# Sums of squares on TensorE, and more products around the start of the output stage, in a two-layer state-space kernel

## The chip, the cores and the metric

The kernel runs on one core of a Trainium2 chip. The metric is the device time of one execution in microseconds (us), as the median of several runs. A core has five engines with a queue each: TensorE (PE, with its weight loads as PEld), VectorE (DVE), ScalarE (ACT), GpSimd (POOL) and SyncE (SP, which here issues most DMAs). Each engine takes its instructions in the order of the program. An instruction that waits for another engine holds back all that stands behind it in its own queue.

## The reference, cut to what matters

The input is `x` of shape (8, 64, 64, 96): 8 images. Two layers follow each other, each of the same form, with different details in the scan.

```python
# layer: x + ref(_gn(x), ...)
xz = x @ in_proj_w                       # 96 -> 2 * 192: x_val and z
x_val = silu(conv3x3_depthwise(x_val) + conv_b)
y = sum over four directions of scan(x_val)   # rows, columns, and both reversed
m = jnp.mean(y, -1, keepdims=True)            # over the 192 channels
v = jnp.var(y, -1, keepdims=True)
y = (y - m) * rsqrt(v + eps) * ln_g + ln_b
return (y * silu(z)) @ out_proj_w             # 192 -> 96, then added to x
```

What the change touches is the last part: mean and variance over 192 channels, the gate with `silu(z)`, and the output product.

## The kernel before, in words

Channels lie on partitions: the 192 channels are two halves of 96 partitions, positions (4096 per image) lie along the free axis. For each image `b` the program runs `scan_rows` (the four scans of layer 1, in 384 sets of 128x1024, with the convolutions of the next image worked in beside them), and then `between(b)`, which calls `out_phase`, the output stage. From image 1 on, `scan_rows` ends with the short unit: 6 sets of 128x960 that belong to layer 2 of the image before. Their results are collected on PE in `collect` (line 1025, 32 small products for a set) and taken off by ACT in `release` (line 1068). PSUM holds one bank for these sums (`pacc`), so that a group's products wait until ACT has taken the group before. The last image's stage is called from `finish`, and a final one of 8 chunks ends the program.

`out_phase` works on chunks of 512 positions: 8 of layer 1's image and, from image 1 on, 8 of layer 2's image before, so 16 chunks in a stage. It is a software pipeline written out by hand. In step k each entry `(stage, lag)` of the tuple `order` (line 1654) does its part for chunk k - lag:

- `first_sum` (lag 0, POOL, line 1620): `y_sum`, the sum of the two halves, 96x512.
- `mean` (lag 1, PE, line 1544): a product with `w["avg"]`, 96x96 of 1/192, which sums over the channels and leaves the mean on all partitions of the PSUM tile `ps_mean`.
- `centre` (lag 1, DVE, line 1636): subtracts it in place.
- `square` (lag 2, ACT, line 1599): squares of both halves to `sq` (2 buffers).
- `second_sum` (lag 2, POOL, line 1627): adds the two halves of `sq` to `squares` (4 buffers).
- `variance` (lag 3, PE, line 1577, at every fourth chunk): four products with `w["avg"][:, :32]`, one for each chunk of a group, into 32 partitions each of the bank `ps_var`.
- `roots` (ACT, line 1650 for the table load, 1651 and 1652) and `newton` (DVE, lines 1537 to 1539), for each group of four: the reciprocal root.
- `row` (lag 8, PE, line 1554): spreads it over the partitions; `scale` (lag 8, DVE, line 1640).
- `gates` (lag 7, PE, line 1567): two products for z into `ps_z` (2 banks); `silu` (lag 7, ACT, line 1616).
- `affine` (lag 9, ACT line 1605, DVE line 1608), `product` (lag 9, POOL, line 1632), `project` (lag 10, PE, line 1589), `end` (lag 10, DVE, line 1752 or 1677), `store` (lag 11).

Within a step each engine takes its parts in the order of the tuple. Behind them come the stages of a plan: the next image's first projections (`ps_proj`, line 577), its first step sizes (`ps_dt`, line 628 on PE; lines 640 to 657 on ACT; three adds of 96x1024 on DVE, lines 661 to 663; a product on POOL, line 607), the scaling and patching of layer 2's sums (ACT line 1772, DVE line 1776), and statistics (DVE line 174). Small banks hold `ps_mean`, `ps_proj`, `ps_dt` and `ps_zb`: two banks in turn.

The first `y_sum` of a stage lies where tiles of the scan lay, and so it waits until PE has read the last set's `out`.

Of the kernel before, what the change touches and what calls it, by code (L numbers as in the profile page):

```python
# [9 lines left out]
F32 = mybir.dt.float32  # L10
AF = mybir.ActivationFunctionType
ALU = mybir.AluOpType
# [4 lines left out]
NB, HH, WW, C = 8, 64, 64, 96  # L17
L = HH * WW
NH = 2
# [4 lines left out]
MM = 512  # L24
SUB = T // MM
P = 128
Q = 4
GC = 32
GS = P // GC
NG = C // GC  # L30
NS = N // GS
# [3 lines left out]
PE_ROWS = 40  # L35
AHEAD = 5
SETS = 4
PER = NG * NS
HEAD = 160
HN = K * HEAD  # L40
# [12 lines left out]
def two_ss2d_layers(ctx: ExitStack, tc: tile.TileContext, t: dict, out: bass.AP):  # L53
# [13 lines left out]
    nc = tc.nc  # L67
# [19 lines left out]
    w = {}  # L87
# [20 lines left out]
    for i in range(L // MM):  # L108
        at = slice(i * MM, (i + 1) * MM)
# [315 lines left out]
    def scan_rows(xc, y, parts, plan, rows, beside):  # L425

        with (
            tc.tile_pool(name="loads", bufs=2, side="right") as loads,
            tc.tile_pool(name="piece", bufs=1) as piece,
            tc.tile_pool(name="work", bufs=2) as work,
            tc.tile_pool(name="pslot", bufs=2, space=PSUM) as pslot,  # L440
            tc.tile_pool(name="pdrive", bufs=1, space=PSUM) as pdrive,
            tc.tile_pool(name="pacc", bufs=1, space=PSUM) as pacc,
            tc.tile_pool(name="pmisc", bufs=1, space=PSUM) as pmisc,
        ):
            units, jobs, sets, x_dbl = parts
            total = len(sets)
            whole = sum(not s["unit"]["short"] for s in sets)
            plan = plan(pmisc)
            with tc.manual_schedule():
                state = None  # L450
                arena = piece.tile([P, 4 * T], F32, name="arena")
                ring = work.tile([P, SETS, T], F32, name="set", bufs=1)
                tables = loads.tile([P, 2 * NS, T], F32, name="bc_rep", bufs=1)
                cums = cycle(tables[:, i, :] for i in (1, 3, 2, NS + 1))
                plan.setdefault(-1, []).insert(0, lambda: low_rows(x_dbl, units[1], rows))
                for n in range(-AHEAD, max(total + 4, max(plan, default=0) + 1)):
                    at = lambda i: sets[n + i] if 0 <= n + i < total else None
                    m, j = divmod(n + 1, PER)
                    if j == 0 and 0 <= m < len(jobs):

                        stages = []
                        if m + 2 < len(jobs):
                            prepare = short_ready if jobs[m + 2]["unit"]["short"] else ready_by_time
                            stages += prepare(xc, x_dbl, jobs[m + 2], arena, pmisc)
                        if m % NH == 1 and m // NH + 2 < len(units):
                            unit = units[m // NH + 2]
                            project = short_projection if unit["short"] else projection
                            stages += project(xc, x_dbl, unit, rows, pmisc)
                        for step, stage in stages:
                            plan.setdefault(n + step, []).append(stage)  # L470
                    fetch(at(AHEAD), False, loads, None)
                    if at(0) and at(0)["unit"]["nth"] == 0 and at(0)["first"]:
                        state = piece.tile([P, D // GC * NS], F32, name="state0", bufs=2)
                    advance_set(at(0), state, ring, tables)
                    fill(at(1), pslot)
                    drive(at(2), pdrive)
                    release(at(-4), y, beside)
                    keep_state(at(-1))
                    gate(at(1), pdrive)
                    early(at(1), True, ring)  # L480
                    read_out(at(-1), work)
                    early(at(2), False, ring)
                    replicate(at(4), x_dbl, tables, ("b", 0), ("b", 1))
                    replicate(at(3), x_dbl, tables, ("c", 0), ("b", 3))
                    replicate(at(2), x_dbl, tables, ("c", 1), ("b", 2))
                    replicate(at(1), x_dbl, tables, ("c", 2))
                    replicate(at(0), x_dbl, tables, ("c", 3))
                    replicate_short(at(4), "b", tables[:, 0, :])
                    if n + 4 == whole:
                        fetch(at(4), True, loads, cums)  # L490
                    replicate_short(at(3), "c", tables[:, NS, :])
                    if n + 3 != whole:
                        fetch(at(3), True, loads, cums)
                    late = (n + 1) % NS == 0
                    if not late:
                        collect(at(-3), xc, y, pacc)
                    for stage in plan.pop(n, []):
                        stage()
                    if late:
                        collect(at(-3), xc, y, pacc)  # L500
                assert not plan
# [512 lines left out]
    def collect(s, xc, y, pacc):  # L1014
# [32 lines left out]
        for acc, at in parts:  # L1047
# [6 lines left out]
                skip_group_check=True,  # L1054
            )

    def release(s, y, beside):

        if not s or s["i"] < NS - 1 and not s["unit"]["short"]:
            return  # L1060
        unit, h, g = s["unit"], s["group"]["h"], s["group"]["g"]
        if unit["short"]:
            if h == g == 0:
                ys_far[unit["b"]] = dram.tile([NH, P, NG * HEAD], F32, name="ys_far", bufs=2)
            if g == 0:
                unit["y"] = beside.tile([P, MM], F32, tag="conv_out", name="y_short")
            part = unit["y"][:, g * HEAD : (g + 1) * HEAD]
            nc.scalar.mul(part, s["group"]["acc"][:, :HEAD], 0.5)
            if g == NG - 1:
                nc.sync.dma_start(ys_far[unit["b"]][h], unit["y"][:, : NG * HEAD])  # L1070
            return
        n = T // Q
        for a in range(Q):
            yk = positions(
                y[GC * g : GC * (g + 1), h, :], unit["column"], unit["t0"] + a * n, n
            )
            acc = s["group"]["acc"][GC * a : GC * (a + 1), :n]
            nc.scalar.copy(yk, like(acc, unit["column"]))  # L1078
# [397 lines left out]
    def out_phase(*streams, plan=None, brief=None):  # L1476
# [9 lines left out]
        with (  # L1486
# [8 lines left out]
            n = len(streams) * chunks  # L1495
            brief = brief or pool
# [8 lines left out]
            held = [{} for _ in range(n)]  # L1505
# [35 lines left out]
            def mean(c):  # L1541
                held[c]["mean"] = pmm.tile([P, MM], F32, tag="mm", name="ps_mean")
                ps = held[c]["mean"][:C, :]
                nc.tensor.matmul(ps, w["avg"], held[c].pop("sum"), start=True, stop=True)  # L1544

            def row(c):

# [22 lines left out]
            def variance(c):  # L1570

                if c % Q < Q - 1:
                    return
                group = groups[c // Q]
                group["var"] = pvar.tile([P, MM], F32, name="ps_var")
                for q in range(Q):
                    nc.tensor.matmul(
                        group["var"][GC * q : GC * (q + 1), :],
                        w["avg"][:, :GC],
                        held[c - Q + 1 + q].pop("squares"),  # L1580
                        start=True,
                        stop=True,
                        skip_group_check=True,
                    )

            def project(c):
                held[c]["out"] = po.tile([P, MM], F32, name="ps_out")
# [7 lines left out]
                    )  # L1595

            def square(c):
                held[c]["sq"] = brief.tile([C, NH, MM], F32, name="sq", bufs=2)
                nc.scalar.activation(held[c]["sq"], part(c), AF.Square)  # L1599

            def affine(c):
# [16 lines left out]
            def first_sum(c):  # L1618
                held[c]["sum"] = brief.tile([C, MM], F32, name="y_sum", bufs=2)
                nc.gpsimd.tensor_tensor(  # L1620
                    held[c]["sum"], part(c)[:, 0, :], part(c)[:, 1, :], ALU.add
                )

            def second_sum(c):
                sq = held[c].pop("sq")
                held[c]["squares"] = brief.tile([C, MM], F32, name="squares", bufs=Q)
                nc.gpsimd.tensor_tensor(  # L1627
                    held[c]["squares"], sq[:, 0, :], sq[:, 1, :], ALU.add
                )

            def product(c):
# [16 lines left out]
            def roots(group):  # L1648
# [3 lines left out]
                nc.scalar.activation(group["r"], group["r"], AF.Exp, scale=-0.5)  # L1652

            order = (
                (load, 6), (mean, 1), (row, 8), (gates, 7), (variance, 3), (project, 10),
                (square, 2), (affine, 9), (silu, 7), (store, 11),
                (first_sum, 0), (second_sum, 2), (product, 9),
                (centre, 1), (scale, 8), (end, 10),
            )
            with tc.manual_schedule():  # L1660
# [302 lines left out]
    with rotating():  # L1963
        ps = psum.tile([P, T], F32, tag="ps", name="ps_flag")
# [96 lines left out]
```

## Time and profile before

| what | value |
|---|---|
| runs | 11935.63, 11943.43, 11960.0 us; median 11943.43 us |
| profiled execution | 11940.1 us, span 11938.2 us |
| busy share of the span | DVE 91%, POOL 89%, ACT 76%, PE 73% |
| granted PE clock over the span | 0.757 of full speed |
| `squares` on POOL (line 1627) | 128 instructions, 175.7 us |
| `ps_var` on PE (line 1577) | 256 records, 48.9 us |
| `ps_mean` on PE (line 1544) | 256 records, 190.7 us |

The profiled execution is read as one run, 3.3 us under the median. A product of these shapes stands in the trace as two records of TensorE, each with a weight load ahead of it. The clock column (PEclk) is the share of full TensorE clock that was granted in a stretch; in this kernel it changes between 0.50 and 1.00 only. An idle time in brackets behind a row names the engine's instruction that ended it.

The eight output stages that follow the scans, from the first `y_sum` to the next scan's first set, take about 100 us (image 0), 140.5 us (images 1 to 5), 145 us (image 6) and 170 us with its tail (the last image); the final one of 8 chunks takes 70 us.

### The profile page before, as it was taken

The page shows a single profiled execution, that of the slowest core. Times are in us where ns is not written, and L with a number is a line of the kernel's source. Part 1 is how long each engine was busy: PE and PEld are TensorE (multiplying, and loading weights), DVE is VectorE, ACT ScalarE, POOL GpSimd, SP SyncE. Part 2 cuts the span into 40 slices and gives each one's busy share as a digit, 9 for nine tenths or more (in the row PEclk, how much of TensorE's full clock was granted, in tenths as well). Part 3 has the DMA queues.
Part 4 walks back from the last instruction along what each step waited for, and adds up shares of the span by engine and source line. Part 5 has one row for each costly group of instructions (what it writes and reads, how often), then busy time and mean ns, then how long its engine had stood idle before and what let it go on. Part 6 is the DMA issues. An engine that isn't in the chain of part 4 may idle for free. (4 is left out here: it accounts for less than half of the span.)

```text
span 11938.2 us, 146996 instructions
## 1 busy us (share of the span) xinstructions
PE 8683.2 (73%) x50950; PEld 3939.2 (33%) x50950; DVE 10805.3 (91%) x6095; ACT 9034.2 (76%) x14768; POOL 10622.2 (89%) x4799
## 2 busy tenths in 40 slices
PE   6865578776777777776787777877777776886557
PEld 2332233332333323333233332333233332333222
DVE  8999899997999979999799997999879998899985
ACT  6777678786787777877778777787777877777775
POOL 6999889996999979999799987999879998799984
PEclk7776677777778777778777777777778777777667
DMA  4444344444445545445454445444544545444442
GB/s 132 154 165 156 127 163 167 164 156 155 157 165 166 169 140 171 161 159 168 138 171 164 169 150 158 162 159 167 166 146 166 168 158 168 139 159 164 157 151 64
DMA packets 670703, 1862.39 MB, mean 156 GB/s; under 512 B 186728, under 2 KB 201486, under 8 KB 669949
## 3 DMA queue, kind: packets, MB, share of 16 engines
q1 hardware_dynamic: 662781, 1840.30, 46.6%
q10 hardware_dynamic: 7168, 12.59, 0.3%
q8 instruction: 405, 6.64, 0.2%
q14 instruction: 349, 2.86, 0.1%
HBM read 1539.34 MB, written 313.28 MB: 155 GB/s over the span
## 5 line engine op out<-in xcount | busy, mean ns | idle before, releaser
L1012 POOL TENSOR_TENSOR out<-set,bc_rep 128x1024 f32<-128x1024 f32 x3120 | 7318.1, 2368 | 622.4 <-DVE set L996 529.8
L996 DVE TENSOR_TENSOR_SCAN set<-decay,state,set 128x1024 f32<-128x1024 f32 x2304 | 5323.3, 2340 | 310.0 <-ACT decay L943 164.4
L943 ACT ACTIVATE decay<-dt_rep,w_a 128x1024 f32<-128x1024 f32 x3072 | 3420.1, 1114 | 1295.0 <-DVE set L996 1290.9
L1048 PE MATMUL acc<-out,w_gather 128*32 128x256 f32 x24576 | 2396.1, 517 | 23.9 <-POOL out L1012 23.6
L1115 PE MATMUL ps_conv<-edged,taps 96*96 96x512 f32 (+1 forms) x4032 | 2196.7, 688 | 19.2 <-DVE arena L869 10.8
L969 POOL TENSOR_TENSOR set<-dtu_rep,bc_rep 128x1024 f32<-128x1024 f32 (+1 forms) x816 | 1965.5, 2409 | 49.5 <-DMA dtu_rep<-dtu_short 27.5
L996 DVE TENSOR_TENSOR_SCAN set<-decay,set 128x1024 f32<-128x1024 f32 x768 | 1731.2, 2281 | 132.4 <-ACT decay L943 73.6
L981 DVE TENSOR_TENSOR set<-drive,bc_rep 128x2048 f32<-128x2048 f32 x768 | 1743.5, 2270 | 36.5 <-DMA bc_rep<-x_dblr 25.8
L731 PE MATMUL ps_sp<-w_eye,arena 128*96 128x128 f32 x7680 | 1130.6, 310 | 595.5 <-ACT arena L743 500.3
L1039 PE MATMUL acc<-map,w_eye 96*32 96x256 f32 x4608 | 577.3, 584 | 1317.5 <-ACT map L1078 855.9
L1078 ACT COPY map<-acc 32x256 f32<-32x256 f32 x3072 | 1473.8, 480 | 69.9 <-PE acc L1048 29.4
L1048 PEld LDWEIGHTS acc<-out,w_gather 128*32 128x32 f32 x24576 | 877.7, 140 | 1401.8 <-issue 1038.1
L731 PEld LDWEIGHTS ps_sp<-w_eye,arena 128*96 128x96 f32 x7680 | 980.4, 145 | 905.2 <-ACT arena L743 619.4
L697 PE MATMUL ps_dt<-w_dtw,x_dbl 7*128 7x96 f32 x3840 | 820.4, 378 | 570.9 <-ACT arena L743 457.3
L1115 PEld LDWEIGHTS ps_conv<-edged,taps 96*96 96x96 f32 (+1 forms) x4032 | 699.9, 188 | 1286.8 <-issue 1226.8
L697 PEld LDWEIGHTS ps_dt<-w_dtw,x_dbl 7*128 7x128 f32 x3840 | 715.9, 275 | 816.3 <-ACT arena L743 526.3
L983 DVE TENSOR_TENSOR set<-drive,bc_rep 128x1024 f32<-128x1024 f32 x768 | 921.9, 1200 | 23.4 <-DMA bc_rep<-x_dblr 12.0
L961 ACT COPY drive<-dtu_rep 128x1024 f32<-128x1024 f32 x768 | 777.9, 1013 | 112.4 <-DMA dtu_rep<-dtu_far 84.9
L708 ACT ACTIVATE arena<-ps_dt 128x384 f32<-128x384 f32 x480 | 235.5, 491 | 558.6 <-PE ps_dt L697 543.8
L1039 PEld LDWEIGHTS acc<-map,w_eye 96*32 96x32 f32 x4608 | 104.1, 125 | 1639.8 <-ACT map L1078 1002.9
L607 POOL TENSOR_TENSOR arena<-arena,map 96x1024 f32<-96x1024 f32 x240 | 634.7, 2644 | 7.3 <-ACT arena L743 7.2
L1007 ACT COPY state<-set 128x1 f32<-128x1 f32 x2304 | 422.2, 183 | 6.8
(207 smaller groups left out, 7910.9 us busy)
## 6 DMA issues: line engine op xcount, KB each, us to landing
dt_rep<-dt_far SPq DMA_DIRECT2D x768, 512.0 KB
dtu_rep<-dtu_far SPq DMA_DIRECT2D x768, 512.0 KB
bc_rep<-x_dblr SPq DMA_DIRECT2D x512, 512.0 KB
bc_rep<-x_dblc SPq DMA_DIRECT2D x512, 512.0 KB
dt_far<-arena SPq DMA_DIRECT2D x240, 384.0 KB
dtu_far<-arena SPq DMA_DIRECT2D x240, 384.0 KB
xc_far<-conv_out SPq DMA_DIRECT2D x224, 192.0 KB
dt_rep<-dt_short SPq DMA_DIRECT2D x48, 480.0 KB
```

Of the source, the lines that this page charges most:

```text
L697: nc.tensor.matmul(job["ps"][:, j, :], unit["x_dbl"][: R + 1, at : at + P], w["dtw0"][:, k, h * C : (h + 1) * C], start=True, stop=True,)
L731: nc.tensor.matmul(job["ps"][:C, j * P : (j + 1) * P], job[name][:, s * BLOCKS + j, :], w["whole_eye"], is_transpose=True, start=i == 0, s ...
L943: nc.scalar.activation(s["decay"], s["group"]["dt"], AF.Exp, scale=rate)
L961: nc.scalar.copy(s["group"]["drive"], s["group"]["dtu"])
L969: nc.gpsimd.tensor_tensor(s["buf"], s["group"]["dtu"], b, ALU.mult)
L981: nc.vector.tensor_tensor(ring[:, :2, :], drive, tables[:, :2, :], ALU.mult)
L983: nc.vector.tensor_tensor(s["buf"], s["group"]["drive"], unit["b", i], ALU.mult)
L996: nc.vector.tensor_tensor_scan(ordered(s["buf"], unit), ordered(s["decay"], unit), ordered(s["buf"], unit), 0.0 if unit["nth"] == 0 else s ...
L1012: nc.gpsimd.tensor_tensor(s["out"], s["buf"], s["unit"]["c", s["i"]], ALU.mult)
L1048: nc.tensor.matmul(acc, w["gather"], s["out"][:, at : at + n], start=False, stop=s["i"] == NS - 1, skip_group_check=True,)
L1078: nc.scalar.copy(yk, like(acc, unit["column"]))
L1115: nc.tensor.matmul(job["ps"][:C, :], taps[l][:k, h, tap, :], edged[:k, tap // 3 : tap // 3 + rows, tap % 3 : tap % 3 + WW], start=tap == 0 ...
```

## The change

It has four parts. `second_sum` is dropped: the variance's products take both halves of `sq` and add them in PSUM, 8 products for a group instead of 4, and `sq` gets 4 buffers. `variance` moves to the front of PE's step, ahead of `mean`, `row` and `gates`. For the first six chunks of every output stage the product of `mean` is made a second time, into a bank of `ps_z` that nobody reads. And a new function `warm` makes three products of 128x128 by 128x512 from a set's `out`, after the last whole set has been advanced: in the last three steps in which sets are collected, once for each of the last three sets.

```diff
+WARM = 6
...
                     if not late:
                         collect(at(-3), xc, y, pacc)
+                    if n >= total:
+                        warm(at(-3), pmisc)
                     for stage in plan.pop(n, []):
                         stage()
                     if late:
...
+    def warm(s, pmisc):
+
+        if not s:
+            return
+        ps = pmisc.tile([P, MM], F32, tag="mm", name="ps_warm")
+        for _ in range(NS - 1):
+            nc.tensor.matmul(ps, w["whole_eye"], s["out"][:, :MM], start=True, stop=True)
...
             def mean(c):
                 held[c]["mean"] = pmm.tile([P, MM], F32, tag="mm", name="ps_mean")
                 ps = held[c]["mean"][:C, :]
-                nc.tensor.matmul(ps, w["avg"], held[c].pop("sum"), start=True, stop=True)
+                total = held[c].pop("sum")
+                nc.tensor.matmul(ps, w["avg"], total, start=True, stop=True)
+                if c < WARM:
+                    again = pz.tile([P, MM], F32, name="ps_z")[:C, :]
+                    nc.tensor.matmul(again, w["avg"], total, start=True, stop=True)
...
+                for h in range(NH):
+                    for q in range(Q):
+                        nc.tensor.matmul(
+                            group["var"][GC * q : GC * (q + 1), :],
+                            w["avg"][:, :GC],
+                            held[c - Q + 1 + q]["sq"][:, h, :],
+                            start=h == 0,
+                            stop=h == NH - 1,
+                            skip_group_check=True,
+                        )
                 for q in range(Q):
-                    nc.tensor.matmul(
-                        group["var"][GC * q : GC * (q + 1), :],
-                        w["avg"][:, :GC],
-                        held[c - Q + 1 + q].pop("squares"),
-                        start=True,
-                        stop=True,
-                        skip_group_check=True,
-                    )
+                    del held[c - Q + 1 + q]["sq"]
...
-                held[c]["sq"] = brief.tile([C, NH, MM], F32, name="sq", bufs=2)
+                held[c]["sq"] = brief.tile([C, NH, MM], F32, name="sq", bufs=Q)
...
-            def second_sum(c):
-                sq = held[c].pop("sq")
-                held[c]["squares"] = brief.tile([C, MM], F32, name="squares", bufs=Q)
-                nc.gpsimd.tensor_tensor(
-                    held[c]["squares"], sq[:, 0, :], sq[:, 1, :], ALU.add
-                )
...
             order = (
-                (load, 6), (mean, 1), (row, 8), (gates, 7), (variance, 3), (project, 10),
+                (load, 6), (variance, 3), (mean, 1), (row, 8), (gates, 7), (project, 10),
                 (square, 2), (affine, 9), (silu, 7), (store, 11),
-                (first_sum, 0), (second_sum, 2), (product, 9),
+                (first_sum, 0), (product, 9),
```

## The prediction

> **What bounds the kernel now.** I read the page's shares first: DVE 91%, POOL 89%, PE 73% at a granted clock of 0.757. These are averages; the scans, which the change leaves alone, are DVE's and POOL's. So I took the timeline around the stage that follows image 1's scans, first `y_sum` at 2828.97 us, and ask there what ends each wait. Clock and work by stretch, cut where the clock changes (columns: stretch, its length, then busy us of PE, PEld, DVE, ACT, POOL with instructions, granted clock, DMA share, GB/s):
>
> ```profile
> 2801.00:2835.10 34.10, 11.91 (x206) 7.20 (x199) 19.04 (x18) 22.19 (x47) 26.26 (x14) 0.50 0.66 209
> 2835.10:2841.90 6.80, 6.17 (x15) 1.60 (x13) 3.65 (x3) 3.37 (x4) 5.01 (x5) 1.00 1.10 217
> 2842.00:2859.00 17.00, 12.84 (x24) 3.48 (x24) 7.88 (x8) 12.69 (x17) 8.25 (x7) 0.50 0.82 203
> ...
> 2873.32:2889.70 16.38, 16.38 (x26) 4.16 (x27) 9.15 (x10) 9.11 (x12) 9.72 (x6) 0.50 0.25 75
> 2889.70:2920.50 30.80, 28.68 (x79) 9.75 (x77) 27.95 (x40) 27.84 (x38) 22.87 (x15) 1.00 0.24 74
> 2920.50:2930.70 10.20, 9.70 (x13) 2.88 (x14) 9.44 (x10) 4.76 (x7) 6.00 (x4) 0.50 0.20 59
> ```
>
> The stage lasts 139 us, 55 of them at half clock. PE is the bound where it is busy all the time (2873 to 2931), DVE at 2862 to 2873. A half-clock product takes 2.02 us (two records of 0.85), a full-clock one 1.02 (0.43). Now the timeline at the start and in two later steps (start, length, engine, line, work, idle before):
>
> ```profile
> 2823.60 1.08 PE L1025 MATMUL acc<-out,w_gather 128*32 128x160 f32 x32 [0.51 <-ACT y_short L1068]
> 2826.06 1.08 PE L1025 MATMUL acc<-out,w_gather 128*32 128x160 f32 x32 [1.37 <-ACT y_short L1068]
> 2827.64 1.08 PE L1025 MATMUL acc<-out,w_gather 128*32 128x160 f32 x32 [0.51 <-POOL out L1012]
> 2828.97 2.48 POOL L1620 TENSOR_TENSOR y_sum<-map 96x512 f32<-96x512 f32 x2 [1.46 <-PE acc L1025]
> 2830.28 2.02 PE L1544 MATMUL ps_mean<-y_sum,w_avg 96*96 96x512 f32 x2 [1.55 <-POOL y_sum L1620]
> ...
> 2848.87 1.94 PE L1577 MATMUL ps_var<-squares,w_avg 96*32 96x512 f32 x8
> 2850.93 1.26 POOL L1627 TENSOR_TENSOR squares<-sq 96x512 f32<-96x512 f32 x1 [4.42 <-PE ps_var L1577]
> 2850.95 0.69 ACT L1651 ACTIVATE r<-ps_var,eps_ln 128x512 f32<-128x512 f32 x1 [2.46 <-PE ps_var L1577]
> ...
> 2866.71 2.17 DVE L662 TENSOR_TENSOR ln<-ln,z 96x1024 f32<-96x1024 f32 x1
> 2867.76 2.24 POOL L1627 TENSOR_TENSOR squares<-sq 96x512 f32<-96x512 f32 x1
> ...
> 2884.89 1.26 POOL L1627 TENSOR_TENSOR squares<-sq 96x512 f32<-96x512 f32 x1 [6.17 <-PE ps_var L1577]
> ```
>
> The first `y_sum` follows 0.25 us behind PE's last read of `out`: the stage hangs on PE there. The variance stops both ACT and POOL.
>
> **When the clock changes.** From the trace I cut time into the 3.41 us steps in which the clock record moves, and took for each the share of the 128x128 array in use (active rows times columns, times streaming time). After a half-clock step with share 0.7 or more and PE busy 85% or more, the next was at full clock 267 times of 267; with share 0.45 to 0.6 and busy under 96%, 26 of 275. A full-clock step with share under 0.24 was followed by full clock 4 times of 435, with 0.4 or more 972 of 972. So dense products bring the clock back soon, and thin ones lose it even without a gap.
>
> The Trainium skill, TensorE: Matmul & The Clock Gate, Part 1, says that about 3.4 us of sustained work free the clock and one idle window of that length takes it back. The trace differs: 16.38 busy us of 16.38 stayed at 0.50, and the clock fell at 2842 behind a step with no gap over 0.4 us. By the rule the clock would hold from 2835 to the idle stretch at 2851, so the second means would be cost alone (six, 0.86 us each, 5 us an image), and the stretch from 2873 would lose 3 to 7 us to half clock in either kernel.
>
> **1. The idle products, images 1 to 7.** In the changed program's order six of them stand between the fourth group of `collect` (ends 2824.68) and the fifth, three behind the sixth, and the first `y_sum` now waits for the last of these, since it lies where `out` lay. Six are 12 records: 10.2 us at half clock, 5.2 at full. They fill the array, so the clock should come after 2.7 to 6.1 us, say 4.4: 4.4 + (10.2 - 4.4)/2 = 7.3. The fifth group then starts at 2832.1 instead of 2826.06, +6.0; a hole of 1.37 is already taken off. Groups five and six take 2.66 from start to end now and some 1.75 at full clock; three more products add 2.6 and a wait of 0.1. `y_sum` comes at 2836.6 instead of 2828.97: **+7.6** (bounds: full clock at once +5.5; never +13.9). Behind the products wait ACT's last two `y_short` and the whole stage; DVE is idle then anyhow.
>
> **2. Image 0** has no short unit: three groups of products stand between sets that arrive 2.3 us apart, and push the last `collect` and ACT's copies by about +4.
>
> **3. Inside the stage, from the first `y_sum` on.** *Steps 0 to 6.* PE is at full clock, but up to the last `ps_zb` it streams ten products and four more second means one behind the other, 12 us from 1.3: `ps_zb` ends at 13.3, where it ends at 13.5 now. `variance` follows the second `ps_dt`: 17.0 to 19.1 (16 records at full clock, twice 1.06) instead of 19.9 to 21.8. But with 4 buffers `square` of chunk 4 must wait until the variance has read chunk 0, and the table load stands behind it: 19.1 + 1.05 + 1.28 + 1.3 puts the end of the root at 22.8 instead of 23.3. **-0.5.** The idle gap before chunk 6's mean stays at 4 us, so the clock falls again.
> *Steps 7 to 9.* `squares` is gone from POOL; the three adds of lines 661 to 663 (1.48 + 2.17 + 2.17, beside POOL) should take 1.22 each, as the same add took at 2924.85 without it: **-2.1**.
> *Step 10.* The variance's 16 records cost 3.9 us at half clock instead of 1.94, ahead of mean, row and gates, and `square` of chunk 8 with `affine` behind it on ACT wait for them. POOL no longer waits 6.17 us with `product` behind. The eight dense half-clock products should bring the clock back at 48 us after the first `y_sum`; now it comes at 60.7. PE would be 5.5 us early at the first `project`; ACT becomes the bound, at the next `silu` 2.0 us early, and its waits of the next 28 us sum to 3.3. I take -5 in all by step 13.
> *Steps 14 and 18.* Variance ahead of `gates` puts `silu` and the root back by the added 1.06 each: +2.1. The half-clock stretch at 2920 costs PE about 4.5; its cause, a PE gap of 3.1 us behind DVE, shrinks to 2.3, which saves the clock in about one case of three: -1.4. Sum: -5 + 2.1 - 1.4 = **-4** (bounds: +1 if the clock comes back no sooner, -12 if PE stays at full clock through, since 25 of its 55 half-clock us are bound by it).
>
> SP's queue keeps its order; its late loads hide behind steps 0 to 5. The removed 175.7 us of POOL are worth what stands above, no more: POOL waits in the stage.
>
> **Sum.** Images 1 to 6: 6 x (7.6 - 4) = 22. Image 7: 7.6 - 2 = 5.6; its stage runs at full clock from 22.6 us on, so there is less to win. Image 0: 4 - 4 = 0. Final stage, 8 chunks, no idle products: its second means at half clock delay `y_sum` (which waits for them, 1.7 each), its POOL alternation ends: 0. Together +27 on the profiled 11940.1: 11967; the median lies 3.3 above, so **11970**.
>
> **Rivals.** *The clock holds (faster).* The inner gain is 12, not 4: 7 x (7.6 - 12) = -31, 11913. For it: PE bounds 2873 to 2931. Against it: DVE's 5.8 us of adds and the gap after step 6 empty PE. It decides from an inner gain of 11. *The head start is all that changes (slower).* The added variance and second means eat the gains: 7 x 7.6 + 4 = +57, 12000. For it: PE is 93% busy at full clock from 2889 to 2920. *The idle products do not raise the clock,* so the change doesn't do what it says: 7 x 13.9 and no inner gain, +97, 12040. Against it: 267 of 267.
>
> **How the numbers follow.** About 0.2%, 24 us, is what a measurement can tell from no change. Chances: forecast 0.40, clock holds 0.25, head start alone 0.28, no clock 0.07. The forecast lies just past the edge, so four tenths of it count as no change, as does a quarter of the faster case and an eighth of the third: faster 0.19, same 0.26, slower 0.55. The range runs from the faster rival, 11913, to near the last, 12035; the forecast's own is 11945 to 12000.
>
> **What would show it.** In the changed profile: the first `y_sum` some 7.6 us later behind the fourth group of `collect`, with `ps_warm` as its releaser; `square` waiting for `ps_var`; lines 661 to 663 near 1.22; full clock by 50 us into the stage. I am wrong if the stage from first `y_sum` to the next scan shrinks by 10 us or more, or if the idle products take under 5 us of path.

## The result, and the profile after

The changed kernel takes 12012.31 us (median of 4 runs, 11998.8 to 12027.06), the kernel before 11939.53 us on the same chip (11930.0 to 11960.0). The ratio is 1.0059 with a 95% interval of 1.0041 to 1.0077: slower by 0.6%, 73 us. The profiled execution took 12011.98 us, its span is 12009.9 us, 71.7 more than before.

Where the 71.7 us lie is read from both traces with the same division of each of the nine output stages. The *head* goes from the end of the last scan to the start of the first `mean` on PE, the *body* from there to the next scan's first set (or to the program's end), and the *rest* is the scans. Summed over the stages:

| us | before | after | difference | predicted |
|---|---|---|---|---|
| head | 53.7 | 111.1 | +57.3 | +57 |
| body | 1264.9 | 1276.8 | +11.9 | -30 |
| rest | 10619.6 | 10622.1 | +2.5 | 0 |
| half clock between first `y_sum` and next scan | 529 | 399 | -130 | less |

The whole head start was predicted to within 1 us; the gain inside the stage did not come. The loss of the body is uneven: the stages of images 1 and 3 take 6.6 and 5.7 us more, those of images 2, 4 and 5 stay within 0.7 us of the kernel before. The timeline of the changed kernel at the stage behind image 1's scans, with the columns as before (start, length, engine, line, work, idle before and what ended it):

```profile
2817.97 1.08 PE L1028 MATMUL acc<-out,w_gather 128*32 128x160 f32 x32 [0.51 <-ACT y_short L1079]
2818.98 4.13 PE L1066 MATMUL ps_warm<-out,w_eye 128*128 128x512 f32 x6
2823.26 2.81 PE L1066 MATMUL ps_warm<-out,w_eye 128*128 128x512 f32 x6 [0.15 <-PE ps_warm L1066]
2826.01 0.66 PE L1028 MATMUL acc<-out,w_gather 128*32 128x160 f32 x32
2827.20 0.66 PE L1028 MATMUL acc<-out,w_gather 128*32 128x160 f32 x32 [0.54 <-ACT y_short L1079]
2827.80 2.84 PE L1066 MATMUL ps_warm<-out,w_eye 128*128 128x512 f32 x6
2830.86 2.48 POOL L1638 TENSOR_TENSOR y_sum<-map 96x512 f32<-96x512 f32 x2 [8.99 <-PE ps_warm L1066]
...
2849.11 3.64 PE L1593 MATMUL ps_var<-sq,w_avg 96*32 96x512 f32 x16
2852.81 1.06 ACT L1617 ACTIVATE sq<-map 96x1024 f32<-96x1024 f32 x1 [6.19 <-PE ps_var L1593]
2856.55 1.27 POOL L1638 TENSOR_TENSOR y_sum<-map 96x512 f32<-96x512 f32 x1 [7.92 <-PE ps_z L1559]
...
2877.08 3.64 PE L1593 MATMUL ps_var<-sq,w_avg 96*32 96x512 f32 x16
2880.74 1.06 ACT L1617 ACTIVATE sq<-y 96x1024 f32<-96x1024 f32 x1 [5.44 <-PE ps_var L1593]
```

From the fourth `collect` group's end to the first `y_sum` pass 11.8 us (2819.05 to 2830.86); before it was 4.3 (2824.68 to 2828.97). Six idle products run from 2818.98 to 2826.07, with the clock rising on the way, groups five and six take 0.66 us each, three more products follow, and `y_sum` waits for the last. The first two of the stage's four variance groups take 3.64 us, the half-clock price of 16 records, and ACT's `square` stands behind each. In the whole kernel before, POOL's `squares` waited 75.7 us for the variance; now ACT's `square` waits 70.0 us for it, so the wait has changed its engine rather than gone. The waits of POOL's `y_sum` in the page's groups (busy us, mean ns, then idle before and what ended it):

```profile
L1638 POOL TENSOR_TENSOR y_sum<-map 96x512 f32<-96x512 f32 x72 | 90.7, 1264 | 198.1 <-PE ps_z L1559 122.3 <-PE ps_warm L1066 55.3 <-DMA y<-xc_far 7.9
L1593 PE MATMUL ps_var<-sq,w_avg 96*32 96x512 f32 x512 | 83.1, 779 | 0.0
L1066 PE MATMUL ps_warm<-out,w_eye 128*128 128x512 f32 x144 | 81.5, 710 | 1.1 <-PE ps_warm L1066 0.6
```

The same `y_sum` group idled 32.7 us in the kernel before. Now 55.3 us end with an idle product and 122.3 with a second mean (`ps_z`, line 1559); the variance is busy for 83.1 us instead of 48.9. The clock by stretch (columns as before):

```profile
2801.00:2821.50 20.50, 6.77 (x131) 4.85 (x132) 13.45 (x12) 15.18 (x33) 18.31 (x9) 0.50 0.62 201
2821.50:2845.40 23.90, 21.34 (x112) 8.41 (x111) 4.86 (x4) 6.34 (x10) 7.92 (x7) 1.00 0.61 154
2845.40:2859.10 13.70, 13.70 (x29) 3.41 (x28) 6.14 (x6) 7.42 (x11) 2.52 (x2) 0.50 0.70 180
...
2869.30:2889.80 20.50, 17.94 (x36) 4.20 (x35) 13.92 (x14) 9.90 (x14) 9.55 (x5) 0.50 0.27 80
2889.80:2934.20 44.40, 39.16 (x111) 13.16 (x110) 37.02 (x52) 37.62 (x51) 19.91 (x11) 1.00 0.22 65
2934.20:2947.90 13.70, 13.69 (x30) 3.63 (x31) 6.59 (x8) 3.69 (x8) 6.53 (x3) 0.50 0.33 100
```

The idle products do bring the clock, 9.3 us ahead of the first `y_sum`, and it holds until 2845.5. That is 14.6 us into the stage, before the first variance, and in the kernel before it fell at 13.0. The second variance falls into the next half-clock stretch, and so does the stage's last one (2937.80, 3.64 us again), where PE is busy all the time. Image 3 is like it. In images 2, 4 and 5, whose stages are about as long as before, the second variance starts at full clock, which is lost during it (2.67, 3.04 and 2.69 us), and the last one takes 1.92 us at full clock.

What follows takes the change apart. Each run below lists its median, its ratio to the kernel before on the same chip with the 95% interval, and the differences of head and body from the kernel before's profile. The border between a stage and the next scan is not sharp, so a few us move between body and rest from run to run (rest: -12 to +6; in one run -28).

### The profile page after: what moved, and what is told of

It is laid out like the page before. It is cut to its first block, busy times and chain, and to the rows that moved or that the text cites. A ratio compares the mean times of both kernels' runs of the same rounds, so it can differ in the third digit from the quotient of the medians.

```text
span 12009.9 us, 147838 instructions
## 1 busy us (share of the span) xinstructions
PE 8796.1 (73%) x51458; PEld 3982.9 (33%) x51458; DVE 10774.0 (90%) x6095; ACT 9030.2 (75%) x14768; POOL 10440.7 (87%) x4671
## 3 DMA queue, kind: packets, MB, share of 16 engines
q1 hardware_dynamic: 662781, 1840.30, 46.5%
## 5 line engine op out<-in xcount | busy, mean ns | idle before, releaser
L984 DVE TENSOR_TENSOR set<-drive,bc_rep 128x2048 f32<-128x2048 f32 x768 | 1743.7, 2270 | 35.0 <-DMA bc_rep<-x_dblr 23.4
```

Of the source, the lines that this page charges most:

```text
L984: nc.vector.tensor_tensor(ring[:, :2, :], drive, tables[:, :2, :], ALU.mult)
```

## Experiments: the three parts, each removed and each alone

**Without the idle products**

```diff
-                    if n >= total:
-                        warm(at(-3), pmisc)
```

> The changed kernel without its idle products; second means and variance as changed. The profile of the changed kernel put the first y_sum later by 3.8 us (image 0) and 5.5 to 8.4 us (images 1 to 7), 57 us in all, and the rest of the stages longer by 13 us in all. Theory A, plain delay: nothing behind the first y_sum depends on the idle products, so the 57 come back: 12012 - 57 = 11955 (within 10), and the rest of the stages stays within 1 us of the changed kernel's. Theory B, they pay part of it back inside the stage, since without them the first six doubled means run at half clock: the rest of the stage is longer by 3 us or more, and the time is 11975 or above. The prediction's own theory stands with B, at 4 us an image.

11982.69 us, ratio 1.0045 (1.0031 to 1.0059); head +6.7, body +44.1. Theory B: the head start comes back, but the body is 32 us longer than in the changed kernel. So inside the stages the idle products earn 32 of the 51 us that they cost ahead of them, 4.6 us an image over the seven images that have them in the short unit. The total time says less: it falls by 29.6 us without them, so that 21 of the 51 are earned; the rest of the program differs by 11 us between the two profiles, and this was not followed up.

**Without the second means**

```diff
-WARM = 6
+WARM = 0
```

> The changed kernel with each mean made once; idle products and variance as changed. In the changed kernel each y_sum of steps 2 to 5 waits for a second mean, and the clock fell at 15 us into the stage in five images of seven, hardly later than in the kernel before (13 to 14 us). Theory A, the second means only lengthen the first steps, by 0.5 to 1 us a step: without them 3 to 4 us an image come back, about 11985. Theory B, they keep the clock up and so earn what they cost: without them the clock falls within 10 us of the first y_sum, the first variance stays at half clock, and the time is 12012 or above.

12010.25 us, ratio 1.0066 (1.0053 to 1.008); head +57.2, body +13.6. Theory A is wrong by 25 us. B's time is nearly met, its reason is not: in images 1 to 5 the clock falls 11.6 to 12.3 us behind the first `y_sum`, where it fell near 15 in four of them, and the first variance runs at half clock in both kernels, but for image 4 of the changed one. Beside the other two parts the second means cost what they earn.

**The variance part alone** (both edits above)

> The variance part alone: no second sums, products of both halves at the front of PE's step, four sq buffers; no idle products, no second means. Theory A, what POOL gives up PE takes at half clock: the second variance takes 2.7 to 3.9 us instead of 1.9, ahead of mean, row and gates, and steps that get faster thin PE out, which costs the clock once more near the stage's end; the stage from the first y_sum on is within 2 us of the kernel before, 11930 to 11955. Theory B, the prediction's: POOL's freed time shortens the stage by 4 us an image, so 11913 or below.

11975.31 us, ratio 1.0031 (1.0019 to 1.0044); head -0.4, body +31.2. Both theories are too low; the prediction's is off in sign. Stages of images 1 to 5 take 147 to 150 us from the first mean on, instead of 142. The timeline of image 2's stage (first `y_sum` at 4296.0):

```profile
4313.93 3.64 PE L1591 MATMUL ps_var<-sq,w_avg 96*32 96x512 f32 x16
4317.63 1.06 ACT L1615 ACTIVATE sq<-map 96x1024 f32<-96x1024 f32 x1 [5.71 <-PE ps_var L1591]
...
4342.49 3.64 PE L1591 MATMUL ps_var<-sq,w_avg 96*32 96x512 f32 x16
4346.15 1.06 ACT L1615 ACTIVATE sq<-y 96x1024 f32<-96x1024 f32 x1 [5.53 <-PE ps_var L1591]
```

Two variances of an image lie in half-clock stretches, at 1.7 us over the 1.94 of the kernel before, and the next mean, row and gates stand behind each. That is 3.4 us of the 4.7 to 7.6 by which the stages of images 1 to 5 grow.

**The idle products alone** (the kernel before with `warm` and its call)

> The kernel before with the idle products alone. Theory A, plain delay: the first y_sum comes 57 us later in sum over the eight stages and the stage behind it is as long as before: 11940 + 57 = 11997 (within 10). Theory B, the clock that they bring to the first steps shortens the stage behind by 2 us or more an image: 11983 or below. A clock that fails to come (half clock at the first mean) would give 12030 or above.

11981.89 us, ratio 1.004 (1.0026 to 1.0054); head +57.0, body -9.0. Theory B: images 1 to 5 are 1.8 to 3.1 us shorter behind the first mean. The 9 us are a sixth of what the products cost; by the total time (42 us above the kernel before) 15 of the 57 come back.

**The second means alone** (the kernel before with them)

> The kernel before with the second means alone. In the two kernels that differ in them only, without idle products, they added 7 us in the median (11975 to 11983), and the stages of images 1 to 3 and 5 became 3 to 4 us longer while those of image 6 and the final one became shorter. Theory A, they are near to nothing on the whole: 11935 to 11960, the first steps longer by 2 to 5 us (each y_sum waits for a second mean at half clock), with a clock that lasts no longer. Theory B, they bring or hold the clock and shorten the stage: 11925 or below.

11979.78 us, ratio 1.0034 (1.002 to 1.0048); head +4.4, body +42.5. Both theories are wrong: the second means are the dearest part inside the stage. The timeline of image 2's stage shows why (first `y_sum` at 4290.1):

```profile
4313.15 1.91 PE L1548 MATMUL ps_z<-y_sum,w_avg 96*96 96x512 f32 x2
...
4315.00 1.94 PE L1581 MATMUL ps_var<-squares,w_avg 96*32 96x512 f32 x8
...
4317.06 1.26 POOL L1631 TENSOR_TENSOR squares<-sq 96x512 f32<-96x512 f32 x1 [6.19 <-PE ps_var L1581]
...
4318.29 1.26 POOL L1624 TENSOR_TENSOR y_sum<-map 96x512 f32<-96x512 f32 x1
```

At half clock the second mean of the sixth chunk stands ahead of the first variance; POOL's `squares` waits for the variance, and behind `squares` stands the eighth `y_sum`, 28.2 us into the stage instead of 23.4. Where the variance part has taken `squares` off POOL this chain is gone: there the second means add 13 to the body (44.1 against 31.2), not 42.

## Experiments: what in the variance part costs

**Variance at its old place, behind gates**

```diff
-                (load, 6), (variance, 3), (mean, 1), (row, 8), (gates, 7), (project, 10),
+                (load, 6), (mean, 1), (row, 8), (gates, 7), (variance, 3), (project, 10),
```

> The variance part alone as in the run before (second sums dropped, 16 records for a group), but with variance behind gates in PE's step, where it stood. Theory A, the doubled records at half clock are the cost (3.64 us for a group instead of 1.94, twice an image), wherever they stand: 11960 to 11985. Theory B, the place at the front is the cost, since mean, row and gates wait for the variance there: 11950 or below.

12006.24 us, ratio 1.0058 (1.0041 to 1.0075); body +72.7. Theory B is wrong; A's direction holds, with more than it put. With 16 records a group the front place saves 41.5 us of body: behind gates ACT's squares wait 166.8 us for the variance (in 21 waits), at the front 90.2 (in 22). Who waited for the variance's products (us, times), behind gates and then at the front:

```profile
  ACT sq L1615: 166.8, 21
```

```profile
  ACT sq L1615: 90.2, 22
```

**Half of the products**

```diff
-                for h in range(NH):
+                for h in range(1):
...
-                            start=h == 0,
-                            stop=h == NH - 1,
+                            start=True,
+                            stop=True,
```

> The variance part alone, at the front, but with products of the first half of the squares only, 8 records for a group as in the kernel before; the second half of the sum of squares is left out. POOL has nothing to add, and PE no more to do than before. Theory A, the doubled records are the cost: the variance takes 1.9 us again at half clock and the stages are 3.4 us shorter or more than with 16 records, 11950 or below. Theory B, the cost is that the steps get thinner on PE when POOL is out of the way, so that the clock falls once or twice more: it falls here too (near 77 and 122 us into the stage), and the time stays at 11960 or above.

11932.94 us, ratio 0.9993 (0.9984 to 1.0003); body -11.0. Theory A: 8 records instead of 16 take 42.2 us off the body. The clock still falls near 75 and 119 us in image 2, as B has it (images 1, 3 and 4 have falls at 92 and 106 us instead), but that does not decide the time. Against the kernel before the time itself is no change that stands clear of the noise.

**The order alone** (the kernel before with the new order, `second_sum` kept)

> The kernel before with variance at the front of PE's step and nothing else changed; POOL still adds the halves. Theory A, the place costs little: 11930 to 11955. Theory B, the place is the cost, 1.9 us of mean, row and gates waiting at half clock twice an image and the clock lost by it: 11960 or above.

11957.55 us, ratio 1.0014 (1.0004 to 1.0023); body +21.5. Between the two theories: with POOL's adds kept and 8 records a group, the front place costs.

The last two with the variance part alone give a chain from the kernel before, in us of body: order +21.5, POOL's adds dropped at the same number of records, with `sq` from 2 to 4 buffers, -32.5 (21.5 to -11.0), records doubled +42.2 (-11.0 to +31.2). In medians, each less the kernel before on its chip, the steps are +14.8, -24.6 and +45.6. POOL's freed time is worth something, and PE pays more for it. The steps hold in this order only: half of the products at the old place was not run, and with 16 records the front place saves time instead of costing it.

## Experiments: a variance that costs PE little

**Squares in bfloat16, eight buffers** (on the variance part alone)

```diff
+    w["avg16"] = const.tile([C, GC], mybir.dt.bfloat16, name="w_avg16")
+    nc.gpsimd.memset(w["avg16"], 1.0 / P)
...
-                            w["avg"][:, :GC],
+                            w["avg16"],
...
-                held[c]["sq"] = brief.tile([C, NH, MM], F32, name="sq", bufs=Q)
-                nc.scalar.activation(held[c]["sq"], part(c), AF.Square)
+                held[c]["sq"] = brief.tile([C, NH, MM], mybir.dt.bfloat16, name="sq", bufs=2 * Q)
+                nc.scalar.activation(held[c]["sq"], part(c), AF.Square, scale=math.sqrt(P / D))
```

> The variance part alone, at the front, with the squares stored in bfloat16 (scaled so that the weight is 1/128) and eight sq buffers: all 8 products of a group are made, but in one pass each, so that PE has less to do for them than in the kernel before, and no square waits for a variance. Idle products and second means are left out. Theory A, the doubled records at half clock are what the variance part costs (the run with half the products had stages 40 us shorter in sum than the one with all): 11905 to 11940. Theory B, a PE with less to do loses the clock more often: it falls at least once more in each stage than in the kernel before, and the time is 11950 or above.

11883.78 us, ratio 0.9956 (0.9941 to 0.9971): faster than both kernels, by 0.44% against the one before. Body -43.1, more than theory A put. Image 2's stage (first `y_sum` at 4273.7), and the group on the page:

```profile
4291.68 1.04 PE L1593 MATMUL ps_var<-sq,w_avg 96*32 96x512 bf16 x8
...
4315.11 1.04 PE L1593 MATMUL ps_var<-sq,w_avg 96*32 96x512 bf16 x8
```

```profile
L1593 PE MATMUL ps_var<-sq,w_avg 96*32 96x512 bf16 x256 | 28.7, 539 | 0.0
```

All 8 products of a group now take 1.04 us in the half-clock stretches, where the 16 records took 3.64, and 28.7 us in the whole program instead of 90.8. Theory B's further loss of the clock does not show in images 1 to 5, where it falls three times a stage as in the kernel before (in image 2 at 13, 37 and 95 us, before at 14, 41 and 92); only the last image's stage has two falls more.

The Trainium skill, FP8 and Floating Point Precision, TensorE Precision Notes, says that a true FP32 product takes four passes through the array. The runs agree in the main: 3.64 / 1.04 = 3.5.

**The same with four buffers**

> The same as the run with bfloat16 squares and eight buffers, but with four sq buffers, so that the square of a group's first chunk waits until the variance of the group before has been made. Theory A, the wait is paid: ACT stands still for it twice or more an image, 10 us or more above the run with eight buffers. Theory B, the wait is hidden behind the centred input that the square needs anyway: within 6 us of it.

11880.96 us, ratio 0.9957 (0.9941 to 0.9973); head -9.0, body -25.7, rest -28.4. Theory B: ACT's wait for the variance (37.9 us in 14 waits, none with eight buffers) costs nothing on the whole. The body is 17 us longer than with eight buffers, and the head and the rest are shorter by more; why was not tried.

**Everything, with bfloat16 squares** (the changed kernel with them, eight buffers)

> The changed kernel with idle products and second means, but with bfloat16 squares and eight sq buffers. Theory A, once the variance is cheap only the head start is left: the first y_sum 57 us later in sum, of which the warm first steps give back 9 (the idle products alone moved the stages so), 11970 to 11990. Theory B, the idle products pay for themselves once PE is not held by the variance: 11950 or below.

11937.26 us, ratio 0.9996 (0.9987 to 1.0005); head +56.2, body -45.5. The time is B's, the reason is neither: what the idle products and second means add to the bfloat16 variance is 53.5 us (11937.26 less 11883.78), all of it head (56.9 in the profiles); in the body they give back 2.4. A's number was too high because the cheap variance was worth more than the half-products run had shown. This kernel has the least half clock of all, 358 us, and is no faster than the one before; the run with eight buffers has 455.

**The kernel before with bfloat16 `squares`** (POOL writes them; 4 products a group, old place)

> The kernel before with the sums of squares stored by POOL in bfloat16 (scaled as in the other bfloat16 runs): POOL still adds the halves, the variance keeps its 4 products and its place behind gates, but makes them in one pass. Theory A, the gain of the bfloat16 runs (56 to 59 us) is POOL's freed time and the place at the front, with PE's records only out of the way: here most of it is missing, 11920 or above. Theory B, the gain is the cheap variance itself, which no longer holds ACT and POOL: 11905 or below.

11919.42 us, ratio 0.9988 (0.9979 to 0.9997); body -17.9. At the edge of theory A: a cheap variance alone gives some 13 us (4 to 25 by the interval). The other 40 or so of the bfloat16 runs come with the second sums off POOL and the variance at the front; these two were not parted there.

## Why the prediction was right, and where it was not

Right: slower, inside the range of 11913 to 12035. The time, 12012, is 42 us above the forecast of 11970 and outside the forecast's own range; the rival "the head start is all that changes", 12000, came nearest. The whole miss lies in the body, +11.9 instead of -30. So the direction rests on the head, whose mechanism the runs confirm; that the time is inside the range is owed to how far the range reached for its rivals, and is in part luck, since the gain forecast inside the stage was a loss.

- **Step 1 and 2, the idle products.** Predicted 7 x 7.6 + 4 = 57; measured +57.3 in the changed kernel, +57.0 alone. In images 1 to 5 the head grew by 7.5, 8.0, 5.5, 8.4 and 8.0 us, in image 7 by 7.8, in image 0 by 3.8. In image 6 the first `y_sum` itself is not late; its first mean is, by 8.1, since the products stand ahead of it on PE. The rival of no clock is refuted: full clock came 8.3 to 9.3 us ahead of the first `y_sum` in images 1 to 5.
- **Steps 0 to 6: the step that failed first.** It took PE to be at full clock until behind the first variance (17.0 to 19.1, root's end at 22.8). Of images 1 to 5 the clock fell at 14.6 to 15.1 us in four, and held past the variance only in image 4 (29.2). The stage of the kernel before is at half clock for 53.9 us by the clock record (the prediction has 55), and the prediction's 26 of 275 thin steps are those with PE busy 70 to 96%; neither changes the argument. Image 1's variance ran from 18.3 to 21.9 us into the stage, its root ended at 25.7. The wait of `square` for `ps_var` was there as predicted.
- **Steps 7 to 9.** Lines 664 to 666 (661 to 663 before) take 1.21, 1.22 and 1.22 us in image 1's stage, as predicted.
- **Step 10: the term that was mis-sized.** The cost was seen (3.64 us at half clock, predicted 3.9) and called smaller than the gain: -5 by step 13. Measured, the first `project` came 1.1 to 3.8 us earlier in images 5, 2 and 4 and 0.9 and 1.5 later in images 3 and 1, not 5.5 earlier; the clock came back to stay at 53 to 59 us in images 1 to 5, not at 48 (in images 2, 4 and 5 it had been up for one step of 3.4 us from 42.5, 39.4 and 42.4 us on). Taken singly the gain and the cost are -32.5 and +42.2 (with +21.5 for the order); their balance, not their kind, was wrong. The run with bfloat16 squares shows the same from the other side: with the records made cheap the body is 43.1 us shorter than before.
- **Steps 14 and 18.** The predicted +2.1 is too small where gains made earlier are given back there; the lines show this for image 4, for the others it is not shown. In image 4 the clock held through the first variance, and the seventh `project` came 7.0 us earlier than before; the next scan came 0.7 earlier. The timeline near the end of that stage, in the changed kernel and then in the kernel before:

```profile
7370.70 1.12 PE L1569 MATMUL ps_r<-r,w_pick 32*96 32x512 f32 x2 [0.52 <-DVE y L1651]
7371.75 3.73 PE L1582 MATMUL ps_z<-x_in,zw 96*96 96x512 f32 x4
7375.27 3.44 PE L1607 MATMUL ps_out<-y,w_out 96*96 96x512 f32 x4
...
7378.75 0.69 DVE L1688 TENSOR_TENSOR x_in<-ps_out,x_in 96x512 f32<-96x512 f32 x1 [5.42 <-PE ps_out L1607]
```

```profile
7336.25 1.96 PE L1567 MATMUL ps_z<-x_in,zw 96*96 96x512 f32 x4
7338.04 1.88 PE L1589 MATMUL ps_out<-y,w_out 96*96 96x512 f32 x4
...
7339.96 0.69 DVE L1677 TENSOR_TENSOR x_in<-ps_out,x_in 96x512 f32<-96x512 f32 x1 [2.07 <-PE ps_out L1589]
```

  The same eight records of `ps_z` and `ps_out` take 7.0 us instead of 3.7, and DVE waits 5.42 for them instead of 2.07. At full clock PE had been ahead of its inputs there (0.38 and 0.52 us of idle time that DVE ended, the second shown); the clock had just fallen, and 3.3 us went back.
- **Image 7.** Its stage was said to run at full clock from 22.6 us on. That reading was wrong: the kernel before falls to half clock there again at 46.5 us (for 3.4) and at 70.4 us (for 6.8). The body, put at -2, became 2.9 us longer.
- **Second means.** They were put at 0 in the stage and 0 in the final one. In the changed kernel that is so (body +11.9 with them, +13.6 without). Alone they cost 42.5, beside the variance part 13, and nothing only where the idle products are there as well; idle products and second means without the variance part were not run. The parts do not add up: alone their bodies are -9.0, +42.5 and +31.2, together +11.9.

## What to carry to other kernels

Before work moves from a side engine to TensorE, price it at the clock of the stretch where it lands; here the doubled products (17 of 32 groups at half clock in the run with the variance part alone) cost more than the side engine's freed time gave. Idle products that bring the clock are worth only what the work behind them was losing to half clock: here 51 to 57 us paid for 2 to 32 back inside the stages. And less half clock is no gain by itself: the kernel with the least of it was not the fastest, while making the same products cheaper (squares in bfloat16), without idle products and second means, turned the change into a gain of 0.44%.

## What the runs showed of the hardware

- The clock's rule from the trace of before held in the changed kernel: behind a half-clock step of 3.41 us with an array share of 0.7 or more and PE busy 85% or more, full clock followed 282 times of 285; a full-clock step with a share under 0.24 was followed by full clock 8 times of 431, one with 0.4 or more 1025 times of 1025. The Trainium skill, TensorE: Matmul & The Clock Gate, HAM oscillation, names idle gaps of PE of over some 3.4 us as what loses the clock. The fall in image 4's stage at 7371.6 us does not fit: in the 10 us ahead of it the longest gap was 0.52 us, behind products with 32 rows (`ps_r`).
- A group of 8 products of 96x32 by 96x512 takes 3.64 us in float32 and 1.04 us in bfloat16 at half clock.
- Three adds of 96x1024 on DVE, which took 1.48, 2.17 and 2.17 us beside POOL's work, took 1.21, 1.22 and 1.22 us with POOL idle beside them (image 1's stage).
